# Issuing the next pair's norm, gate and channel attention between the groups of the running pair's attention

## The chip, the core and the metric

One core of a Trainium2 chip runs the whole kernel as one program. Its engines work side by side and each takes its own instructions strictly in order: TensorE (PE in the profile; PEld are its weight loads) multiplies matrices into PSUM, VectorE (DVE) and ScalarE (ACT) do elementwise work, GpSimd (POOL) too, and SyncE (SP) issues the DMAs of this kernel. An instruction waits on semaphores for what it needs, and everything behind it on its engine waits with it. PSUM is eight banks of 128 rows by 512 fp32 values. The metric is device time in microseconds (us), the median of several executions; lower is better.

## What is computed

Four layers run one after the other on 8 images of 64 channels and 64 by 64 pixels, in fp32: a selective scan with a gated convolution (layer 0), channel and spatial attention (layer 1), a small network that is trained for two steps inside the kernel (layer 2), and another spatial attention (layer 3). The change is in what the kernel calls its second stage, which is the end of layer 0 and all of layer 1:

```python
# xo: after the scan.  The norm is over the 64 channels of a pixel.
n = channel_norm(xo)                       # (n - mean) / sqrt(var + 1e-6) * g + b
s0..s3 = split(n, 4, channels)             # s_i is max-pooled by 2**i
outs = [upsample(depthwise3x3(s_i), 2**i) for i in 0..3]
x = xo + gelu(mix1x1(concat(outs))) * n    # the gate
energy = x @ x.T                           # 64 x 64, channel attention
out_c = softmax(max(energy) - energy) @ x
q, k, v = wq @ x + bq, wk @ x + bk, wv @ x + bv     # 16, 16 and 64 rows by 4096 pixels
out_s = v @ softmax(q.T @ k).T             # 4096 x 4096, spatial attention
x2 = (gamma_ca * out_c + x) + (gamma_sa * out_s + x)
```

## The kernel before

The stages are four calls in `conv_seq_kernel`. The second is `gate_and_attention` (L1090). It works on pairs of images: two images of 64 channels fill the 128 rows, so a tile `x` of 128 by 4096 holds a pair, and the loop at L1175 runs over four pairs. For each pair three things follow one another.

**The preparation** (L1176 to L1258). `pair_norm` (L127) centres x with a matmul by `cen`, 1024 pixels at a time into a tile of two PSUM banks (`cps`, from the pool `sc`), copies it on VectorE into the bordered tile `pads[0]`, squares it on ScalarE (`sq`) and sums the squares with a matmul into `var` (L144; a bank of the pool `av`). `rstd` comes from VectorE, a ScalarE square root and a VectorE reciprocal. A matmul by `spread` (L156, 16 rows deep) spreads it to all rows (`rps`), VectorE multiplies (L161) and ScalarE scales and shifts (L162). Three rounds of maxima on VectorE (L1188, L1190) fill `pads[1]` to `pads[3]`. `move` (L1134) copies 16 channels at a time with DMAs, six to a tile, so that three rows of the 3 by 3 kernel lie on different partitions of the tiles `mv`; `conv` (L1144) is then three matmuls. The convolutions go from the smallest grid to the largest, each added to the doubled one before it (L1157, L1166); the largest runs in four blocks `j` of 1024 pixels (`cvps0`), each followed by Gelu on ScalarE and a multiplication and an addition on GpSimd (L1219 to L1221). x goes to DRAM (L1225). Then x is transposed (`xTps`), copied (`xT`) and multiplied with itself into `enps` (L1239), and the softmax of the energy becomes the 128 by 128 matrix `cmapT`.

**The projection** (`project`, L852): k and v of the pair into SBUF, from tiles of two banks.

**The attention** (`run`, L884). A block `i` of 512 queries meets 32 blocks `j` of 128 keys, two to a group, so a pair has 8 x 16 = 128 groups, numbered n. Group n issues the scores of its two key blocks (`scores`, L898: matmuls 16 rows deep into a two-bank tile, ScalarE's exponential into `ex`, VectorE's addition into `sum`), and then the products with v of the group before (`values`, L918). At n % 16 = 1 the queries of the next block are made (`qps`), at 2 the block before is divided (`sumps`, a VectorE reciprocal, four more VectorE operations), at 4 it is finished (`fps`, `x2t`, a DMA). There are four `ex` tiles, so two groups' worth.

The order on every engine is made when the program is built: a scheduler follows the order in which the kernel calls things, and pulls an instruction ahead where it reckons that its inputs are there; DMAs are pulled ahead most. [...] PSUM has three pools of two tiles each in this stage: `mm` with single banks (q, `sumps`, `fps`, the small convolutions), `sc` with two banks a tile (scores, `cps`, `rps`, `cvps0`, `xTps`, k, v) and `av` with single banks (`av`, `var`, `enps`). That is all eight banks.

Of the kernel before, what the change touches and what calls it, by code (L numbers as in the profile page):

```python
# [17 lines left out]
NB = 8  # L18
C = 64
# [24 lines left out]
class Common:  # L44
# [81 lines left out]

    def pair_norm(self, work, sc, var, src, dst, consts, eps, g, b):  # L127

        nc = self.nc
        cen, avg, spread = consts
        for i in range(NBK // 2):
            ps = sc.tile([128, 2, BK], F32, name="cps", tag="sc")
            for e in range(2):
                nc.tensor.matmul(
                    ps[:, e, :], cen, src[:, bass.ts(2 * i + e, BK)], start=True, stop=True
                )
            nc.vector.tensor_copy(dst(i), ps.rearrange("p e (r c) -> p (e r) c", c=S))
            sq = work.tile([128, 2, BK], F32, name="sq", tag="blk", bufs=3)  # L140
            nc.scalar.activation(sq, ps, AF.Square)
            for e in range(2):
                m = 2 * (NBK - 1 - 2 * i - e)
                nc.tensor.matmul(  # L144
                    var[: 2 * NBK], avg[:, m : m + 2 * NBK], sq[:, e, :],
                    start=(i + e == 0), stop=(2 * i + e == NBK - 1),
                )
        rstd = work.tile([2 * NBK, BK], F32, name="rstd", tag="rstd", bufs=1)
        nc.vector.tensor_scalar(rstd, var[: 2 * NBK], eps, None, ALU.add)
        nc.scalar.activation(rstd, rstd, AF.Sqrt)  # L150
        nc.vector.reciprocal(rstd, rstd)
        for i in range(NBK // 2):
            ps = sc.tile([128, 2, BK], F32, name="rps", tag="sc")
            for e in range(2):
                j = 2 * (2 * i + e)
                nc.tensor.matmul(  # L156
                    ps[:, e, :], spread[:, j : j + 2, :].rearrange("k e c -> k (e c)"), rstd,
                    start=True, stop=True,
                )
            out = dst(i)  # L160
            nc.vector.tensor_tensor(out, out, ps.rearrange("p e (r c) -> p (e r) c", c=S), ALU.mult)  # L161
            nc.scalar.activation(out, out, AF.Identity, bias=b, scale=g)  # L162
# [644 lines left out]
class Attention:  # L807
# [76 lines left out]
    def run(self, p, x, k, v, finish):  # L884
# [68 lines left out]
        for n in range(len(groups) + 5):  # L953
            now = []
            if n < len(groups):
                i, g = groups[n]
                now = [(i, j, scores(i, j)) for j in (2 * g, 2 * g + 1)]
            for one in ahead:
                values(*one)
            ahead = now  # L960
            if n % per == 1 and n > per and n // per + 1 < NBK:
                queries(n // per + 1)
            if n % per == 2 and n > per:
                done[n // per - 1] = divide(n // per - 1)
            if n % per == 4 and n > per:
                finish(n // per - 1, done.pop(n // per - 1))

# [122 lines left out]
def gate_and_attention(cm, xh, w, a, x1, mixes, x2):  # L1090
# [4 lines left out]
    with ExitStack() as ctx:  # L1095
# [79 lines left out]
        for p in range(NB // 2):  # L1175
            x = io.tile([2 * C, L], F32, name="x", tag="x")  # L1176
            nc.sync.dma_start(x, xh[2 * p : 2 * p + 2].rearrange("b c l -> (b c) l"))

            def inner(i):
                return pads[0][:, 1 + 2 * i * rows : 1 + 2 * (i + 1) * rows, 1 : S + 1]  # L1180

            var = avp.tile([128, BK], F32, name="var", tag="av")
            cm.pair_norm(work, sc, var, x, inner, cn, 1e-6, cn_g, cn_b)
            src = pads[0][:, 1 : S + 1, 1 : S + 1]
            for i in range(1, 4):
                n = S // 2**i
                m = one.tile([2 * C, 2 * n, n], F32, name=f"max{i}", tag=f"wide{n}")
                nc.vector.tensor_tensor(m, src[:, :, 0::2], src[:, :, 1::2], ALU.max)  # L1188
                src = pads[i][:, 1 : n + 1, 1 : n + 1]
                nc.vector.tensor_tensor(src, m[:, 0::2, :], m[:, 1::2, :], ALU.max)  # L1190
                for r, t in enumerate(moved[i]):
                    move(i, part * r, t)
            p3 = bank(8, 8)
            conv(p3, 3, moved[3][0], 0, 8)
            d3 = doubled(p3, 8, 8)
            p2 = bank(16, 16)
# [3 lines left out]
            d2 = doubled(u2, 16, 16)  # L1200
            u1 = one.tile([2 * C, 32, 32], F32, name="u1", tag="u1")
            for i in range(2):
                p1 = bank(16, 32)
                conv(p1, 1, moved[1][i], 0, 16)
                add_doubled(u1[:, 16 * i : 16 * i + 16, :], p1, d2[:, 8 * i : 8 * i + 8, :])
            d1 = doubled(u1, 32, 32)
            for j in range(NBK // 2):
                blk = bass.ts(j, 2 * BK)
                t = moved[0][j % 3]
                move(0, 2 * j * rows, t)  # L1210
                p0 = sc.tile([128, 2, BK], F32, name="cvps0", tag="sc")
                for e in range(2):
                    conv(p0[:, e, :].rearrange("p (r c) -> p r c", c=S), 0, t, e * rows, rows)
                t = work.tile([2 * C, 2 * rows, S], F32, name="gt", tag="blk", bufs=3)
                add_doubled(
                    t, p0.rearrange("p e (r c) -> p (e r) c", c=S),
                    d1[:, j * rows : (j + 1) * rows, :],
                )
                nc.scalar.activation(t, t, AF.Gelu, bias=fb)  # L1219
                nc.gpsimd.tensor_tensor(t, t, inner(j), ALU.mult)  # L1220
                nc.gpsimd.tensor_tensor(  # L1221
                    x[:, blk], x[:, blk], t.rearrange("p r c -> p (r c)"), ALU.add
                )

# [3 lines left out]
            en = avp.tile([128, BK], F32, name="enps", tag="av")  # L1228
            for j in range(TQ // 8):
                ps = sc.tile([128, 8, 2 * C], F32, name="xTps", tag="sc")  # L1230
                for i in range(8):
                    nc.tensor.transpose(ps[:, i, :], x[:, bass.ts(8 * j + i, 128)], cm.ident)
                xT = work.tile([128, 8, 2 * C], F32, name="xT", tag="blk", bufs=3)
                if j % 2:
                    nc.scalar.copy(xT, ps)
                else:
                    nc.vector.tensor_copy(xT, ps)
                for i in range(8):
                    nc.tensor.matmul(  # L1239
                        en[:, : 2 * C], xT[:, i, :], xT[:, i, :],  # L1240
                        start=(j + i == 0), stop=(8 * j + i == TQ - 1),
                    )
            lo, tot = (work.tile([2 * C, 1], F32, name=n, tag=n) for n in ("lo", "tot"))
            for r in halves:
# [9 lines left out]
                )  # L1254
            cmapT = work.tile([2 * C, 2 * C], F32, name="cmapT", tag="cmapT")
            cm.transpose(psum, cmapT, cmap2)
            for e, r in enumerate(halves):
                nc.sync.dma_start(mixes[2 * p + e], cmapT[r, r])  # L1258

# [11 lines left out]
            att.run(p, x, k, v, finish)  # L1271
# [632 lines left out]
```

## Time and profile before

The median of three runs is 12997.07 us (12996.37 to 12998.29). The profiled execution took 12995.36 us; its span, from the first to the last instruction, is 12993.6 us.

| stretch of the span (us) | what | PE busy | DVE busy | ACT busy | mean granted PE clock |
|---|---|---|---|---|---|
| 0 to 7605 | first stage, scan | | | | |
| 7612 to 7720 | preparation of pair 0 | 73.78 | 41.34 | 18.97 | 0.76 |
| 8255 to 8680 | projection and attention of pair 1 | 423.89 | 352.08 | 258.27 | 1.00 |
| 8680 to 8790 | preparation of pair 2, start of its projection | 84.52 | 39.17 | 23.19 | 0.81 |
| 8790 to 9214 | projection and attention of pair 2 | 422.77 | 352.59 | 255.65 | 1.00 |
| 9757 to 12993.6 | third and fourth stage | | | | |

Times of the trace count from the start of the span. In a line of the timeline come the start, the duration of the group of instructions, the engine, the line of the kernel, the operation, what it writes and reads, the shape and the count (x8). A bracket at the end gives the engine's idle time before it and what released it. An fp32 matmul appears as two records, so "x8" of 512 columns are four matmuls. The granted clock is that of TensorE, 1.0 being full speed. A matmul's end is modelled, so starts are the surer reading.

### The profile page before, as it was taken

How to read it: one execution, taken by the hardware profiler on the slowest of the kernel's cores; microseconds unless marked ns; L12 is line 12 of the kernel's file. 1: busy time of each engine (PE TensorE's matmuls, PEld its weight loads, DVE VectorE, ACT ScalarE, POOL GpSimd, SP SyncE). 2: the span in 40 equal slices, each digit the busy share in tenths (PEclk: the TensorE clock that was granted, in tenths of full speed). 3: DMA queues.
4: the chain of work that ended last, by engine and by line, in shares of the span. 5: the costliest groups of instructions: out<-in, count | busy, mean ns of one | idle time of the engine just before them, and what ended most of it. 6: DMA issues, size and time to landing. Idle time of an engine off the chain costs nothing. (4 is left out here: it accounts for less than half of the span.)

```text
span 12993.6 us, 115955 instructions
## 1 busy us (share of the span) xinstructions
PE 11161.9 (86%) x36395; PEld 4115.1 (32%) x36395; DVE 10881.6 (84%) x7636; ACT 7717.6 (59%) x10047; POOL 6754.4 (52%) x3126
## 2 busy tenths in 40 slices
PE   7788888888888888888887779999996768999999
PEld 2233232232232232232232222323324553333332
DVE  5999999999999999999999958677686786766766
ACT  4676675675675666766765536445465674544544
POOL 4877888878888888788788830000003681000000
PEclk8999999999999999999999989999998888999999
DMA  4888888888889888888888830000001100000000
GB/s 164 301 292 291 308 301 293 306 298 303 300 300 309 296 296 308 300 298 305 297 299 304 295 120 6 24 18 11 17 6 66 39 27 23 6 16 17 6 10 6
DMA packets 686280, 2333.69 MB, mean 180 GB/s; under 512 B 98224, under 2 KB 98896, under 8 KB 683088
## 3 DMA queue, kind: packets, MB, share of 16 engines
q1 hardware_dynamic: 685648, 2326.13, 51.8%
q8 instruction: 290, 4.75, 0.1%
q14 instruction: 342, 2.80, 0.1%
HBM read 2240.69 MB, written 76.28 MB: 178 GB/s over the span
## 5 line engine op out<-in xcount | busy, mean ns | idle before, releaser
L614 POOL TENSOR_TENSOR ct<-ct,h 128x1024 f32<-128x1024 f32 x2048 | 4799.6, 2357 | 1447.1 <-DVE h L605 969.2
L642 PE MATMUL yps<-ct,ident 128*128 128x512 f32 x8192 | 4233.9, 652 | 547.3 <-POOL ct L614 545.3
L605 DVE TENSOR_TENSOR_SCAN h<-a,state,bdu 128x1024 f32<-128x1024 f32 x1344 | 3153.8, 2347 | 227.3 <-ACT state L609 26.7
L915 DVE TENSOR_TENSOR sum<-sum,ex 128x1024 f32<-128x1024 f32 x1920 | 2347.9, 1223 | 770.7 <-ACT ex L908 655.6
L908 ACT ACTIVATE ex<-sc 128x1024 f32<-128x1024 f32 x2048 | 1985.1, 1021 | 1529.8 <-PE sc L903 1529.7
L642 PEld LDWEIGHTS yps<-ct,ident 128*128 128x128 f32 x8192 | 1586.9, 205 | 3164.6 <-issue 1959.1
L582 ACT ACTIVATE a<-dt,amat 128x1024 f32<-128x1024 f32 x2048 | 2333.4, 1142 | 18.1 <-POOL dt L535 14.9
L601 DVE TENSOR_TENSOR bdu<-bt,du 128x1024 f32<-128x1024 f32 x1792 | 2194.9, 1225 | 101.4 <-ACT du L561 46.3
L922 PE MATMUL av<-ex,v 128*64 128x512 f32 x8192 | 1987.8, 606 | 0.0
L609 ACT COPY state<-h 128x1 f32<-128x1 f32 x2048 | 382.9, 187 | 2191.1 <-DVE h L605 2189.4
L903 PE MATMUL sc<-q,k 16*128 16x512 f32 (+1 forms) x8192 | 1656.3, 628 | 5.0 <-ACT ex L908 4.4
L605 DVE TENSOR_TENSOR_SCAN h<-a,bdu 128x1024 f32<-128x1024 f32 x448 | 1024.3, 2286 | 83.5 <-ACT state L609 16.7
L922 PEld LDWEIGHTS av<-ex,v 128*64 128x64 f32 x8192 | 498.2, 136 | 1363.9 <-issue 1360.5
L903 PEld LDWEIGHTS sc<-q,k 16*128 16x128 f32 (+1 forms) x8192 | 562.1, 184 | 1078.8 <-ACT ex L908 743.5
L1220 POOL TENSOR_TENSOR gt<-gt,pad 128x1024 f32<-128x1024 f32 x16 | 34.9, 2180 | 1617.5 <-ACT gt L1219 1538.1
L590 POOL TENSOR_TENSOR bt<-bt,dus 128x1024 f32<-128x1024 f32 x256 | 602.9, 2355 | 8.9 <-DMA bt<-bc 8.8
L408 PE MATMUL vps<-pad,convd 128*128 128x512 f32 x1152 | 534.2, 597 | 5.6 <-ACT z L393 5.6
L605 DVE TENSOR_TENSOR_SCAN h<-a,state,bt 128x1024 f32<-128x1024 f32 x192 | 499.5, 2602 | 15.0 <-POOL bt L590 8.2
L1593 DVE RECIPROCAL r<-e 128x512 f32<-128x512 f32 x128 | 420.7, 3323 | 0.0
L637 PE MATMUL yps<-y,ident 128*128 128x512 f32 x384 | 301.7, 917 | 115.6 <-ACT y L623 115.5
L1596 POOL TENSOR_TENSOR r<-r,half 128x512 f32<-128x512 f32 x128 | 162.7, 1271 | 360.9 <-issue 188.0
L582 ACT ACT_TABLE_LOAD x265 | 340.0, 1283 | 4.7
(402 smaller groups left out, 10325.1 us busy)
## 6 DMA issues: line engine op xcount, KB each, us to landing
bt<-bc SPq DMA_DIRECT2D x2048, 512.0 KB
ct<-bc SPq DMA_DIRECT2D x2048, 512.0 KB
x<-x SPq DMA_DIRECT2D x12, 2048.0 KB
bc<-e SPq DMA_DIRECT2D x256, 64.0 KB
zd<-z SPq DMA_DIRECT2D x64, 256.0 KB
z<-zd SPq DMA_DIRECT2D x64, 256.0 KB
x<-x SPq DMA_DIRECT2D x32, 512.0 KB
part<-x SPq DMA_DIRECT2D x128, 128.0 KB
```

What stands on the lines that cost most here:

```text
L408: nc.tensor.matmul(held[0].rearrange("p (r c) -> p r c", c=S), convd[:, t, :], pad[:, j * rows + dy : (j + 1) * rows + dy, dx : dx + S], s ...
L582: nc.scalar.activation(ctl["a", n], ctl["dt"], AF.Exp, scale=amat[:, ctl["k"], n : n + 1])
L590: nc.gpsimd.tensor_tensor(bt, bt, ctl["dus"], ALU.mult)
L601: nc.vector.tensor_tensor(z, bt, ctl["du"], ALU.mult)
L605: nc.vector.tensor_tensor_scan(h[:, flip], a[:, flip], z[:, flip], 0.0 if state is None else state[:, n : n + 1], ALU.mult, ALU.add,)
L614: nc.gpsimd.tensor_tensor(ct, ct, h, ALU.mult)
L642: nc.tensor.matmul(ctl["ps"][:, bass.ts(i, BK)], cm.ident, ct[:, bass.ts(i, BK)], start=False, stop=(n == N - 1),)
L903: nc.tensor.matmul(sc[:, e, :], k[r : r + d, bass.ts(j, 128)], qs[i][r : r + d, :], start=True, stop=True,)
L908: nc.scalar.activation(ex, sc, AF.Exp)
L915: nc.vector.tensor_tensor(sums[i], sums[i], ex, ALU.add)
L922: nc.tensor.matmul(avs[i][r, :], v[:, j, r], ex[:, e, :], start=(j == 0), stop=(j == TQ - 1))
L1593: nc.vector.reciprocal(r[n][s], e[n][:, s])
```

## The change

`pair_norm` and the body of the pair loop down to `cmapT` become a generator, `prepare(p, w, made, at)`, that stops at a `yield` after every small part. The first pair is prepared as before, in one go, with w = 2 (two banks to a tile). For the others, `prepare(p + 1, 1, ...)` is made before the attention of pair p, and `run` calls `between(n)` at the end of each of the 128 groups, which takes it one part further. With w = 1 each tile is one bank of the pool `mm`, so that the score tiles keep theirs. `var` and `enps` are begun only at n % 16 = 4 and take two places of the pool `av`, so that the attention's own `av` tiles keep alternating. What is left of a preparation after the attention would be run through before the next projection.

The parts fall on these groups: the load of x at 0; `cps` with the `var` of the part before at 4 to 11, the last `var` at 12; `rstd` at 13; `rps` with the multiplication and the scaling at 14 to 21; the three rounds of maxima with their moves at 22 to 24; the first two moves of the full grid at 25; the small convolutions at 26 to 29; then for each of four blocks two parts with a convolution and one with Gelu and the GpSimd work, at 30 to 41; `xTps` with the energy of the part before at 52 to 59, the last energy at 60; the softmax at 61; `cmapT` at 62. From 63 to 127 nothing is added.

Small differences besides: with w = 1 the centred x is copied to `pads[0]`, and x transposed to `xT`, on ScalarE each time (before: VectorE, and VectorE and ScalarE in turn). `add_var` and `add_energy` stand one part behind what feeds them, with w = 2 too. The moves for block j of the full grid are called two blocks ahead.

```diff
-    def run(self, p, x, k, v, finish):
+    def run(self, p, x, k, v, finish, between=lambda n: None):
...
             if n % per == 4 and n > per:
                 finish(n // per - 1, done.pop(n // per - 1))
+            if n < len(groups):
+                between(n)
...
+        def tile_of(w, name):
+            if w == 2:
+                return sc.tile([128, 2, BK], F32, name=name, tag="sc")
+            ps = psum.tile([128, BK], F32, name=name, tag="mm")
+            return ps.rearrange("p (w n) -> p w n", w=1)
+
+        def accumulator(name, w):
+            ps = avp.tile([128, BK], F32, name=name, tag="av")
+            if w == 1:
+                avp.tile([128, BK], F32, name=name + "2", tag="av")
+            return ps
...
+        def prepare(p, w, made, at):
             x = io.tile([2 * C, L], F32, name="x", tag="x")
             nc.sync.dma_start(x, xh[2 * p : 2 * p + 2].rearrange("b c l -> (b c) l"))
...
+            while w == 1 and at() != 4:
+                yield
+            var = accumulator("var", w)
...
+            for i in range(NBK // w):
+                ps = tile_of(w, "cps")
+                for e in range(w):
+                    nc.tensor.matmul(
+                        ps[:, e, :], cen, x[:, bass.ts(w * i + e, BK)], start=True, stop=True
+                    )
+                if w == 2:
+                    nc.vector.tensor_copy(inner(i), grid(ps))
+                else:
+                    nc.scalar.copy(inner(i), grid(ps))
+                sqs[i] = work.tile([128, w, BK], F32, name="sq", tag="blk", bufs=3)
+                nc.scalar.activation(sqs[i], ps, AF.Square)
+                if i:
+                    add_var(i - 1)
+                yield
+            add_var(NBK // w - 1)
+            yield
             rstd = work.tile([2 * NBK, BK], F32, name="rstd", tag="rstd", bufs=1)
             nc.vector.tensor_scalar(rstd, var[: 2 * NBK], 1e-6, None, ALU.add)
             nc.scalar.activation(rstd, rstd, AF.Sqrt)
             nc.vector.reciprocal(rstd, rstd)
+            yield
+            for i in range(NBK // w):
+                ps = tile_of(w, "rps")
+                for e in range(w):
+                    j = 2 * (w * i + e)
+                    nc.tensor.matmul(
+                        ps[:, e, :], spread[:, j : j + 2, :].rearrange("k e c -> k (e c)"), rstd,
+                        start=True, stop=True,
+                    )
+                out = inner(i)
+                nc.vector.tensor_tensor(out, out, grid(ps), ALU.mult)
+                nc.scalar.activation(out, out, AF.Identity, bias=cn_b, scale=cn_g)
+                yield
...
-        for p in range(NB // 2):
+        made, place = {}, [0]
+        parts = prepare(0, 2, made, None)
+        for p in range(NB // 2):
+            for _ in parts:
+                pass
+            x, cmapT = made.pop(p)
...
             k, v = att.project(p, x)
-            att.run(p, x, k, v, finish)
+            more = p + 1 < NB // 2
+            parts = prepare(p + 1, 1, made, lambda: place[0]) if more else iter(())
+
+            def between(n, parts=parts):
+                place[0] = n % (TQ // 2)
+                next(parts, None)
+
+            att.run(p, x, k, v, finish, between)
```

The rest of `prepare` holds the lines of before with `yield` between them, in the parts listed above.

## Prediction

> **What bounds the kernel now.** I first cut the span into stretches and read the engines' busy time in each (start:end, length, then PE, PEld, DVE, ACT and POOL busy, granted clock, DMA share, GB/s).
>
> ```profile
> 8145.00:8255.00 110.00, 84.33 (x254) 38.42 (x251) 40.64 (x40) 23.37 (x23) 18.01 (x8) 0.81 0.23 61
> 8255.00:8680.00 425.00, 423.89 (x2186) 130.90 (x2184) 352.08 (x310) 258.27 (x271) 0.00 (x0) 1.00 0.01 5
> ```
>
> In the attention TensorE is never free and at full clock; VectorE is busy 83%, ScalarE 61%. In the preparation nothing is full and the clock falls to 0.81. Next, the timeline where pair 1 begins, for what the change can save:
>
> ```profile
> 8152.72 3.60 PE L136 MATMUL cps<-x,p_cen 128*128 128x512 f32 x8
> ...
> 8254.15 6.17 PE L861 MATMUL kps<-x,sa_wk 128*128 128x512 f32 x14
> ```
>
> From the first `cps` to the first `kps` are 101.4 us. The same two starts are 8682.24 and 8784.56 for pair 2 (102.3), 9211.37 and 9315.50 for pair 3 (104.1): 307.9 in all, 102.6 a pair. Pair 0 stays where it is, and its order on TensorE hardly changes: I cost it at 0 (either end 3 us, for the squares' sums that now stand one part later).
>
> Then the timeline of a group, with the queries of a block behind it:
>
> ```profile
> 8424.94 1.14 PE L903 MATMUL sc<-q,k 16*128 16x512 f32 x8
> 8426.01 1.94 PE L922 MATMUL av<-ex,v 128*64 128x512 f32 x8
> 8427.88 1.12 PE L894 MATMUL qps<-x,sa_wq 128*128 128x512 f32 x2
> 8428.93 1.14 PE L903 MATMUL sc<-q,k 16*128 16x512 f32 x8
> ```
>
> Plain groups take 2.94 and 3.15 us in turn (8403.51, 8406.66, 8409.60), 3.05 on average; with one more matmul 3.99.
>
> **What is added on TensorE.** A 512-column record takes (3.60 - 0.16) / 8 = 0.43 us at full clock. Per pair: `cps`, `var` and `rps` 48 records, 20.6 us; convolutions 60 full records 25.8, six of 256 columns 1.3, six of 64 columns 0.4; transposes 32 x 0.107 ("x8" takes 1.04) = 3.4; energy 64 x 0.115 ("x32" takes 3.84) = 7.4; `cmapT` 0.1. That is 59.0. They come in about 55 runs of one kind; the group above paid 3.99 - 3.05 - 0.86 = 0.08 for its run, `fps` (8438.82 to 8439.88, after a 3.15 group) 0.2; at 0.13 this is 7.2. Together 66 (63 to 70), all on the path, as TensorE has no gap to hide them in. If nothing else happened: 102.6 - 66 = 36 us a pair, 110 in all.
>
> **What makes TensorE wait.** The changed program's own order on each engine shows what stands behind what. I follow it with durations of the trace.
>
> 1. *rstd and scaling, n = 13 to 21.* In the order of ScalarE the scaling of part n stands ahead of the exponentials of group n + 1; it waits for VectorE's multiplication, which stands behind both sums of group n, which wait for its exponentials. That is a ring.
>
> ```profile
> 8140.99 1.94 ACT L908 ACTIVATE ex<-sc 128x1024 f32<-128x1024 f32 x2 [1.21 <-PE sc L903]
> ...
> 8142.05 2.55 DVE L915 TENSOR_TENSOR sum<-sum,ex 128x1024 f32<-128x1024 f32 x2 [0.60 <-ACT ex L908]
> ```
>
> From exponential to sum 1.06, two sums 2.55, multiplication of one bank 0.66 (the same at L337), scaling of one bank 0.81 (L338), handovers 0.1: 5.2 us a turn, against 3.99 for TensorE, whose next scores wait for a score tile that the exponential frees. At n = 13 ScalarE waits for `rstd` between two table loads of 1.28 and VectorE adds a reciprocal of 3.34: from the scores of n = 12 the scaling of part 14 ends at 16.0 us. Then turns: 15, 16, 17 bring it to 31.3; 18 has the block's reciprocal (3.36) in the ring, 39.8; 19 has the division, two range tests and only half an exponential (5.4), 45.2; 20 has `x2t` (0.74), 51.1; 21 ends at 56.3. The scores of group 22 start about 52.5. Unhindered they would start at 4.0 + 3.05 + 8 x 3.99 + 2.7 (q, `sumps`, `fps`) = 41.6. Wait: 11. The maxima (2.29, 1.23, 0.69, 0.43, 0.29, 0.23) then stand between sums, and the four `ex` tiles run out: 2.3 more.
>
> 2. *The moves, n = 26.* Two dozen DMAs lie between the first maxima and the smallest convolution, and SP issues them one by one:
>
> ```profile
> 8184.08 40.48 SPq L1138 DMA_DIRECT2D mv<-pad  x48
> ...
> 8196.65 1.23 DVE L1190 TENSOR_TENSOR pad<-max 128x1024 f32<-128x1024 f32 x1
> ...
> 8214.49 25.90 PE L1148 MATMUL cvps<-mv,fw 128*128 128x64 f32 x60 [14.57 <-DMA mv<-pad]
> ```
>
> 8214.49 - 8197.88 = 16.6 us, of which 24 issues of 0.587 are 14.1; pair 0 has 16.7. The order is the same in the changed program. The first maxima are done 4.9 after the last scaling, so the data are there at +21.4; TensorE gets to that convolution after the products of group 25, at +13.7. It waits 7.7 there, and with it all scores behind. `x2` and `x1` writes stand in the same queue, but nothing is waiting for those.
>
> 3. *Gelu, n = 32, 35, 38, 41.* Table load 1.28, Gelu 1.15, table load 1.28 ahead of the next exponentials, 3.7 us of ScalarE against its 1 us of slack a group. The order puts q, `fps` or a third of a convolution there, which covers part; I get 1, 2, 0.5 and 1: 4.5 (2 to 10). GpSimd's 4.5 us a block (2.18 + 2.35) have no other work beside them and end long before n = 52.
>
> 4. *Softmax at 61* : two exponentials that wait for VectorE's minima and reciprocals ahead of the next group's: 1.5. *Projection*: the k copy on VectorE now stands behind the division of the last block (recip 3.36, then 3 us): first `kps` to first scores 16.7 instead of 15.9, and the sums start later: 1.5.
>
> Hidden: the `cps` parts (ScalarE 0.57 + 0.59 beside 1.9 more of TensorE), `xTps`, the x load (four groups ahead), the sums of the eight convolution parts (2.55 + 0.69 of VectorE beside 5.7 of TensorE). If that cover failed, the eight scaling turns show the size: about 1 us a part.
>
> 5. *The clock.* No long wait stands in an attention of before, so the price has to come from two places. After the 14.6 us wait above TensorE ran at half speed to 8220.7 (records 0.85 apart), 6.2 us, 3.1 lost. And at the start of pair 0's attention:
>
> ```profile
> 7738.09 2.54 PE L903 MATMUL sc<-q,k 16*128 16x512 f32 x8 [1.11 <-ACT ex L908]
> 7740.55 3.68 PE L922 MATMUL av<-ex,v 128*64 128x512 f32 x8
> 7744.17 2.09 PE L903 MATMUL sc<-q,k 16*128 16x512 f32 x8
> 7746.19 3.68 PE L922 MATMUL av<-ex,v 128*64 128x512 f32 x8
> 7749.80 1.14 PE L903 MATMUL sc<-q,k 16*128 16x512 f32 x8
> ```
>
> A few waits of 1.1 between scores were enough for 11 us at half speed, 5.5 lost. The wait of step 2 costs 3 to 5.5; steps 1 to 3 may add spells. I take 6 a pair; from 3 (one short spell) to 23 (all eight turns of the ring at half speed, 5.6 for a plain group at half and 1.8 for the part: 7.4 instead of 5.2, 17.6, and a spell of 5.5).
>
> The Trainium skill, "TensorE: Matmul & The Clock Gate", Part 1 (the HAM clock gate), speaks against this change: after an idle window of about 3.4 us the array runs at half clock until it has been busy for about 3.4 us. By that rule only the wait of step 2 would count, with 3.4 us at half speed and 1.7 lost a pair, and the total would be 13 us lower; the row at 7738 went to half speed after waits of only 1.1 and stayed there 11 us, so I go by the rows.
>
> **Sum**, a pair: + 66 + 11 + 2.3 + 7.7 + 4.5 + 1.5 + 1.5 + 6 = 100.5, - 102.6: - 2.1. Three pairs: - 6. Against the profiled execution's 12995.4 us this is **12990 us** (it lay 1.7 under the median of the runs, far inside what counts). The gain of the overlap is handed back as waits. About 0.2%, 26 us, is what a measurement tells from no change.
>
> **Rivals.**
> *A, the buffers cover the ring.* Two score and four `ex` tiles let TensorE run on; only 66, the wait of 7.7 and a clock spell of 3 stay: 76.7, a gain of 26 a pair, 12918. For it: no waits in the attention now, though each reciprocal of 3.36 delays VectorE. Against it: there only sums stand behind VectorE; here exponentials do. Half of it would be 12955.
> *B, the clock gate decides, slower.* Place: the ring, n = 14 to 21, where a quarter of each turn is idle and the inserted matmuls are 16 rows deep; at 8177.8 to 8191.4 sixteen such records ran at half speed without ending it. Price 23 instead of 6: 117.5 a pair, + 15 each, 13040. It turns the sign from 8 us a pair, and passes 0.2% from 17.
> *C, it doesn't overlap* (the scheduler puts the parts back behind the attention): about 12995; the order speaks against it, the parts stand between the groups.
>
> **Chances.** Forecast 0.43, A 0.26, B 0.29, C 0.02. Faster by over 0.2% 0.26 (A), within 0.2% 0.45 (forecast and C), slower by over 0.2% 0.29 (B). The range takes A's near half and B: 12925 to 13045. The forecast's own range, with 63 to 70 for TensorE and a clock price of 3 to 12, is 12970 to 13020.
>
> **What would show it.** First `cps` of a later pair about 14 us after its predecessor's first scores; `kps` right behind the last `fps`. Groups of 5.2 us at n = 14 to 21, releaser of the scores ACT, of the scaling DVE; one wait of 7 to 8 us for a DMA at the 64-column convolution, then records at 0.85. Attentions of pairs 0 to 2 about 510 us from first scores to last `fps`, pair 3's 410. Wrong would be: groups of 4 us there (A), a granted clock well under 0.95 over n = 13 to 41 (B), waits at `cps` or convolutions of the full grid, or at `av` for `var`.

## The result, and the profile after

The changed kernel takes 12992.65 us (median of 12 runs, 12983.43 to 13004.15), the kernel before in the same comparison 12994.37 us; the ratio is 0.9998, with a 95% interval of 0.999 to 1.0006. The profiled execution has a span of 12982.8 us and a run of 12984.6. Forecast were 12990 us and no difference that can be measured.

The overlap does take place. Where pair 1 begins, the timeline of TensorE (start, length, engine, line, operation, tiles) shows the projection right behind the last `fps`, with no preparation between:

```profile
8246.34 1.12 PE L1337 MATMUL fps<-x,cmapT 128*128 128x512 f32 x2
8247.31 5.31 PE L824 MATMUL kps<-x,sa_wk 128*128 128x512 f32 x12
```

The attention that now holds the parts takes more. The windows view gives pair 1 from its first scores to the end of its last `fps`, and the ring's 40 us within it (start:end, length, then PE, PEld, DVE, ACT, POOL busy, granted clock, DMA share, GB/s):

```profile
8263.58:8776.85 513.27, 501.13 (x2327) 153.41 (x2327) 379.72 (x339) 290.75 (x314) 18.14 (x8) 0.96 0.05 13
8331.00:8371.00 40.00, 38.20 (x145) 11.55 (x144) 27.18 (x29) 19.25 (x22) 0.00 (x0) 0.87 0.22 37
```

Before, the same stretch of pair 1 took 412.33 us. The second line is the one to learn from: in the ring TensorE is busy 38.20 of 40 us, and its clock is 0.87. The stage loses time there, but hardly any of it is idle time. The group of the page that waits for exponentials (busy us and mean ns, then the idle time ahead, with what ended most of it) shows only 21.2 us of that over the whole kernel:

```profile
L867 PE MATMUL sc<-q,k 16*128 16x512 f32 (+1 forms) x8192 | 1700.4, 633 | 21.8 <-ACT ex L872 21.2
```

So I split the three attentions that hold parts (first scores to the end of the last `fps`, pairs 0 to 2) with the windows view in stretches of 5 us: idle is length less PE busy, half speed is PE busy times (1 less granted clock), work is the rest, TensorE's time at full clock. The split is not exact: behind a wait the second half of a group's scores waits once more for its own exponential, and the eight `sc` records then read 2.04 us instead of 1.14, all of it busy (8327.82 in the changed kernel). That part counts as work here. Sums of three pairs, in us:

| kernel | length | idle | half speed | work |
|---|---|---|---|---|
| before | 1241.6 | 3.4 | 5.0 | 1233.3 |
| after | 1536.9 | 37.8 | 54.9 | 1444.1 |

The parts bring 210.8 us of work, 34.4 of idle time and 49.9 of half speed: 295.3. What they replace are the stretches from the first `cps` to the first `kps` in the kernel before, 101.4, 101.0 and 101.1 us, 303.6 in all. That saves 8.3 us. With a slower last attention (+1.6) and three projections of 16.27 instead of 15.94 us (+1.0), the stage from the first `kps` to the end of the last `fps` falls from 2023.9 to 2018.2, by 5.7 us.

The ring is there as forecast. All engines of pair 1, in the group with the queries: multiplication (DVE), scaling behind it (ACT), exponentials behind that, sums behind those, and the next multiplication behind the sums:

```profile
8343.27 0.68 DVE L1216 TENSOR_TENSOR pad<-pad,rps 128x512 f32<-128x512 f32 x1
...
8343.98 0.82 ACT L1217 ACTIVATE pad<-pad,cn_b,cn_g 128x512 f32<-128x512 f32 x1 [1.89 <-DVE pad L1216]
8344.70 1.92 ACT L872 ACTIVATE ex<-sc 128x1024 f32<-128x1024 f32 x2
...
8345.74 2.56 DVE L879 TENSOR_TENSOR sum<-sum,ex 128x1024 f32<-128x1024 f32 x2 [1.79 <-ACT ex L872]
...
8348.21 0.68 DVE L1216 TENSOR_TENSOR pad<-pad,rps 128x512 f32<-128x512 f32 x1
```

From one multiplication to the next is a turn of 4.94 us. The wait for the moves and the half-speed records behind it came as forecast too (TensorE and SP's queue; `sc` takes 2.09 instead of 1.14, `av` 3.68 instead of 1.94):

```profile
8385.53 8.80 SPq L1104 DMA_DIRECT2D mv<-pad  x14
...
8395.87 0.85 PE L1114 MATMUL cvps<-mv,fw 128*128 128x64 f32 x6 [3.19 <-DMA mv<-pad]
8396.65 2.09 PE L867 MATMUL sc<-q,k 16*128 16x512 f32 x8
8398.67 3.68 PE L886 MATMUL av<-ex,v 128*64 128x512 f32 x8
```

The square root stands between two table loads and leaves TensorE waiting 1.52 us at 8327.82; the four Gelus of pair 0 leave 0.31, 0.68, 0.31 and 1.64.

### The profile page after: what moved, and what is told of

It is laid out like the page before. It is cut to its first block, busy times and chain, and to the rows that moved or that the text cites. A ratio compares the mean times of both kernels' runs of the same rounds, so it can differ in the third digit from the quotient of the medians.

```text
span 12982.8 us, 115992 instructions
## 1 busy us (share of the span) xinstructions
PE 11190.4 (86%) x36395; PEld 4103.1 (32%) x36395; DVE 10882.1 (84%) x7642; ACT 7771.6 (60%) x10134; POOL 6755.4 (52%) x3126
## 5 line engine op out<-in xcount | busy, mean ns | idle before, releaser
L577 POOL TENSOR_TENSOR ct<-ct,h 128x1024 f32<-128x1024 f32 x2048 | 4800.9, 2358 | 1445.6 <-DVE h L568 973.4
L886 PE MATMUL av<-ex,v 128*64 128x512 f32 x8192 | 2021.2, 615 | 0.0
L867 PE MATMUL sc<-q,k 16*128 16x512 f32 (+1 forms) x8192 | 1700.4, 633 | 21.8 <-ACT ex L872 21.2
L568 DVE TENSOR_TENSOR_SCAN h<-a,bdu 128x1024 f32<-128x1024 f32 x448 | 1024.6, 2287 | 82.7 <-ACT state L572 16.7
```

The lines of the kernel that those rows point to most:

```text
L568: nc.vector.tensor_tensor_scan(h[:, flip], a[:, flip], z[:, flip], 0.0 if state is None else state[:, n : n + 1], ALU.mult, ALU.add,)
L577: nc.gpsimd.tensor_tensor(ct, ct, h, ALU.mult)
L867: nc.tensor.matmul(sc[:, e, :], k[r : r + d, bass.ts(j, 128)], qs[i][r : r + d, :], start=True, stop=True,)
L886: nc.tensor.matmul(avs[i][r, :], v[:, j, r], ex[:, e, :], start=(j == 0), stop=(j == TQ - 1))
```

## The experiments

Theory after the result: the overlap is worth what the work leaves (303.6 - 210.8 = 93 us) and gives it back as short waits and as half speed behind them. Rivals: the gate halves the clock whatever the waits are; or only TensorE's work counts and there is nothing to win back; or part of the effect has nothing to do with the overlap. Ratios are to the kernel before on the same chip. "Stage" is the time from the first `kps` to the end of the last `fps` in one profiled execution (2023.9 before, 2018.2 after), "idle" and "half" are as in the table above.

| run | median us | ratio, 95% | stage | idle | half |
|---|---|---|---|---|---|
| after | 12992.65 | 0.9998 (0.999 to 1.0006) | 2018.2 | 37.8 | 54.9 |
| e1 | 12970.11 | 0.9979 (0.997 to 0.9988) | 1998.0 | 28.9 | 48.3 |
| e2 | 12962.78 | 0.9977 (0.9967 to 0.9986) | 1987.8 | 28.0 | 37.6 |
| e3 | 12971.14 | 0.9983 (0.9974 to 0.9992) | 2010.0 | 39.9 | 51.2 |
| e4 | 12961.22 | 0.9977 (0.9967 to 0.9988) | 1987.3 | 25.9 | 39.6 |
| e5a | 12972.26 | 0.9984 (0.9975 to 0.9993) | 1996.9 | 37.4 | 38.3 |
| e5 | 12957.40 | 0.9975 (0.9965 to 0.9986) | 1980.9 | 29.7 | 29.2 |
| e7 | 12978.45 | 0.9991 (0.9982 to 1.0) | 2008.5 | - | - |
| e8 | 12977.16 | 0.9988 (0.9979 to 0.9997) | 2003.2 | 45.3 | 36.3 |
| e10 | 12926.02 | 0.995 (0.9937 to 0.9964) | 1952.6 | 18.2 | 18.2 |

Work is 1438.0 to 1445.6 us in every kernel of the table with the overlap. Nearly all that differs between their three attentions is idle time and half speed. Each stage is read from one execution; by their intervals, e7 and e8 are not clearly apart from the changed kernel in time, so what is said of them rests on their traces.

### e7: the same parts without the overlap

```diff
-            parts = prepare(p + 1, 1, made, lambda: place[0]) if more else iter(())
+            parts = prepare(p + 1, 2, made, None) if more else iter(())
...
-                next(parts, None)
+                pass
```

> The changed kernel's parts without the overlap: nothing is issued between the groups, and the whole of the next pair's preparation is issued behind the running pair's attention on double banks, as in the kernel before (the sums of squares and the energies stay one block later, the first two moves of the finest scale stay ahead). Theory: the new order inside the preparation is worth nothing by itself, -5 to +5 us of the kernel before. Rival (part of the gain and loss of the change lies in the reordering of the preparation, not in the overlap): more than 5 us off the kernel before.

The theory fell, the rival holds: 13 us under the kernel before, though the interval just reaches no difference. From the last `fps` of a pair to the first scores of the next are 113.51, 113.27 and 113.43 us instead of 117.20, 116.80 and 116.89, 10.7 in all (the other 4.7 of the stage are the half-speed spell at the start of pair 0's attention, which this execution doesn't have). The last sums of squares tell why. Before:

```profile
8165.85 1.12 PE L136 MATMUL cps<-x,p_cen 128*128 128x512 f32 x2
8169.41 3.46 PE L144 MATMUL var<-sq,p_avg 128*16 128x512 f32 x4 [2.43 <-ACT sq L141]
```

and in e7:

```profile
8169.20 1.89 PE L1180 MATMUL var<-sq,p_avg 128*16 128x512 f32 x4
8171.70 1.89 PE L1180 MATMUL var<-sq,p_avg 128*16 128x512 f32 x4 [0.61 <-ACT sq L1196]
```

Issued one block later, the sums no longer wait 2.43 us for their squares, and don't run at half speed behind that. From the first `cps` to the first `rps` pass 21.47 us instead of 25.05. So the new order is worth some 11 us by the trace and 13 by the medians without any overlap. Against that order the overlap shows no gain: in the one execution profiled of each its stage is 10 us longer (2018.2 against 2008.5), part of it spells at the start of attentions that no edit touches. The medians lie 1.7 and 13 us under the kernel before on the same chip, and their intervals overlap, so a loss isn't shown either.

### e2: the wait for the moves

```diff
                 move(0, 2 * j * rows, moved[0][j])
-            yield
+            for _ in range(5 if w == 1 else 1):
+                yield
             p3 = bank(8, 8)
```

> The changed kernel with four more empty parts between the moves and the smallest convolution, about 17 us of attention in which the transfers can land. Theory: TensorE's waits for mv ahead of the smallest convolution (5.37, 3.19 and 2.63 us in the profiled execution) go, and with them the half-speed records right behind (about 3 us per pair): 11 us of wait and up to 9 us of clock, 11 to 20 us in all. If the half-speed time comes from something else it stays: 11 us. Rival (the wait moves: the later convolutions then wait for their own moves, or the xT stage starts late): 0.

The waits for `mv` are gone and the stage is 30.4 us shorter: 9.8 of idle time, 17.3 of half speed and 4.7 by a last attention that began at full clock, which the edit doesn't touch, less 1.5 that work reads higher. Without the 4.7 it is still more than the 20 at most. The theory holds, with a larger term for the clock; the three waits, 11.2 us together, were worth more than twice their length.

### e1, e4, e5a: opening the ring by the order of issue

```diff
             for i in range(NBK // w):
+                if i > 0:
+                    times(i - 1)
+                if i > 1:
+                    scaled(i - 2)
                 ps = tile_of(w, "rps")
...
-                nc.vector.tensor_tensor(out, out, grid(ps), ALU.mult)
-                nc.scalar.activation(out, out, AF.Identity, bias=cn_b, scale=cn_g)
+                rs[i] = ps
                 yield
```

`times` is VectorE's multiplication and `scaled` ScalarE's scaling of one block. e4 is e1 and e2 together; e5a puts `scaled(i - 2)` ahead of `times(i - 1)` and issues no part in each sixteenth group's third.

> The changed kernel with the scaling ring opened: part n issues the multiplication of block n-1, the broadcast of block n and the scaling of block n-2, so that ScalarE no longer waits for VectorE and VectorE no longer waits for TensorE inside one part. Theory (the ring's turn is set by the chain broadcast, multiplication, scaling, exponentials): the turn falls from 4.95 us to TensorE's about 4.0 us, 8 turns, and the half-speed records inside the ring mostly go with it; the term of 11 us per pair goes, so 7 to 11 us per pair, 20 to 33 us in all below the changed kernel. Rival (the clock gate decides, whatever waits there are): the half-speed time stays or moves to the next pause, 0 to 5 us in all. Rival (only TensorE's added work counts): 0.

> Both edits together: the opened ring, and four more empty parts ahead of the smallest convolution. Theory (the two terms are separate waits): the sum of the two, 30 to 50 us below the changed kernel. Rival (the clock gate decides): much less than the sum, as the half-speed time that is cured in one place shows up in the next, 10 to 20 us. Rival (only TensorE's added work counts): 0.

> The ring alone, opened in the right order: in the trace of e1 every scaling on ScalarE still started within 0.05 us of the end of the next block's multiplication on VectorE (8358.79 after 8358.75), since the scaling of block n-2 was issued behind the multiplication of block n-1 in the same tile. Here the scaling of block n-2 comes first, then the multiplication of block n-1, then the broadcast of block n; and no part is issued in the group of the sums and the reciprocal (each sixteenth group's third), so that the broadcast doesn't wait for a bank behind them. Theory (the ring's chain costs 4.95 us a turn, TensorE's work 4.0): with the chain really open the ring's 8 to 11 us per pair go, 10 us more than e1 in the three pairs, that is 28 to 33 us below the changed kernel. Rival (the half-speed records decide and come with the first pause, whatever the ring does): as e1, about 20 us below the changed kernel. Rival (ring without a price): 0.

All three gained, and none for the reason given. From the first `rps` record of pair 1 to the start of the last block's are 38.0 us in e1 and 38.3 in the changed kernel: the ring is as it was. (In e1's pair 2 they are 35.6, but so they are in e2's pair 1, whose ring is that of the changed kernel: in both, 1.7 us are lost to half speed there instead of 5.1.) The timeline of e5, which has e5a's ring, shows it:

```profile
8325.93 0.68 DVE L1213 TENSOR_TENSOR pad<-pad,rps 128x512 f32<-128x512 f32 x1
8326.64 0.82 ACT L1216 ACTIVATE pad<-pad,cn_b,cn_g 128x512 f32<-128x512 f32 x1 [2.31 <-DVE pad L1213]
8327.36 1.92 ACT L872 ACTIVATE ex<-sc 128x1024 f32<-128x1024 f32 x2
```

8326.64 is the first scaling and 8325.93 the first multiplication of the pair, so it is the same block: the scheduler had drawn the scaling ahead of where the program issues it. My reading of e1, that the next block's multiplication held it back, was wrong as well. What e1 and e5a did was to add parts ahead of the convolutions: e1 has no wait for `mv` left, e5a one of 0.92 us. That is e2's cause as far as the traces show it, and e4 gains no more than e2 alone. In e5a, though, idle time is what it was (37.4), since other waits grew (each pair has one of 2.67 or 2.68 us for an exponential), and its gain is half speed alone (54.9 to 38.3).

### e8: the scaling on an idle engine

```diff
-                nc.scalar.activation(out, out, AF.Identity, bias=cn_b, scale=cn_g)
+                if w == 1:
+                    nc.gpsimd.tensor_scalar(out, out, cn_g, cn_b, ALU.mult, ALU.add)
+                else:
+                    nc.scalar.activation(out, out, AF.Identity, bias=cn_b, scale=cn_g)
```

> One edit on the changed kernel: in the overlapped pairs the scaling by gain and bias goes from ScalarE to GpSimd, which is idle there. The traces of e1 and of the ring kernel after it show that the order of issue did not open the ring: each scaling on ScalarE still ran at the end of the same block's multiplication on VectorE (8326.64 behind 8325.93 + 0.68, turns of 4.5 to 5.0 us). On another engine no exponential stands behind a scaling. Theory (the ring's chain sums, multiplication, scaling, exponentials sets the turn of 4.95 us; TensorE's work is 4.0): the turn falls to 4.0 to 4.3 us and the half-speed records inside the ring go; 7 to 11 us per pair, 20 to 33 us in all, or 10 us more than e1's 20 if e1 gained by its empty parts alone. What it costs: GpSimd's scalings are slower (its multiplications of 1024 elements take 2.3 us), so the maxima start some 2 us later and the wait for mv ahead of the smallest convolution grows by as much. Rival (the half-speed time decides and comes with the first pause ahead of the ring): turns stay above 4.6 us, 0 to 10 us in all.

Now the exponentials start beside the scaling, not behind it:

```profile
8342.42 0.78 POOL L1218 TENSOR_SCALAR pad<-pad,cn_g,cn_b 128x512 f32<-128x512 f32 x1 [3.85 <-DVE pad L1216]
8342.51 1.94 ACT L872 ACTIVATE ex<-sc 128x1024 f32<-128x1024 f32 x2 [1.24 <-PE sc L867]
```

From the first to the eighth broadcast of pair 1 pass 30.9 us instead of 38.3, 4.41 a turn with the queries, `sumps` and `fps` in it; all but 1.4 of the 30.9 is TensorE's own work at full clock. The ring cost 7.4 us a pair, 22 in all, its half speed included. But TensorE now comes to the smallest convolution earlier, and finds the transfers no further:

```profile
8384.28 1.52 PE L1114 MATMUL cvps<-mv,fw 128*128 128x64 f32 x6 [7.53 <-DMA mv<-pad]
```

The three waits are 7.23, 7.53 and 7.71 us instead of 5.37, 3.19 and 2.63: 11.3 of the ring's 22 go back at the next wait, more than I had expected. The stage falls by 15.0. The rival (turns above 4.6) is out.

### e3 and e5: table loads

e3 has `AF.Gelu if w == 2 else AF.Identity`, one word in the Gelu's line.

> Leaves out the Gelu of the three overlapped pairs (Identity with the same bias in its place), so that ScalarE loads no table there but those for the square root; everything else as in the changed kernel. Theory: the term for the table loads goes, 4.5 us per pair by the prediction (2 to 10), 13 us in all (6 to 30). The trace of the changed kernel shows waits of TensorE for ex behind the Gelus of 0.3, 0.7, 0.3 and 1.6 us and one half-speed record, which speaks for the lower end. Rival (the exponentials have enough slack to take the loads): 0 to 5 us in all.

The waits for `ex` at the Gelus go, 2.9 us a pair, but idle time doesn't fall: the waits for `mv` are 7.01, 4.83 and 5.98 us in this execution. The stage is 8.2 us shorter, the median 21. Both lie within the theory's 6 to 30, but the profiled execution is the slowest of its eleven (12987.97), and how much of the 21 is the Gelu's, it doesn't tell.

e5 puts the edits of e5a and e2 together, adds epsilon a part earlier, and issues each Gelu in one part with the next convolution.

> All waits taken out that the traces show and that an order of issue can take out: the ring as in e5a, four empty parts ahead of the smallest convolution as in e2, the addition of epsilon a part ahead of the square root (ScalarE waited 1.0 us for it between two table loads), and each Gelu in one part with the next block's convolution, so that TensorE has 2.8 us more work while ScalarE loads tables. Theory (idle time of 11 to 15 us per pair and half-speed time of 16 to 20 us behind it, both caused by the waits): the overlapped attention falls from 512 us to 490 to 495 us, 50 to 65 us in all below the changed kernel, about 12930 us. Rival (the half-speed time comes whatever the waits): only the idle time goes, 8 us per pair, 25 to 30 us in all, no better than e2 and e4 (about 12962 us).

The rival's number came (12957), as the ring had stayed closed. The paired Gelus leave one wait of 2.62 us in place of 0.31, 0.68, 0.31 and 1.64: the last has no convolution beside it and pays for all.

### e6, e9, e12: what a wait costs

```diff
+            if n < len(groups) and dose(n):
+                pause = self.work.tile([128, L], mybir.dt.bfloat16, name="pause", tag="pause", bufs=1)
+                late = now[-1][2][:, 0:1, :].to_broadcast([128, dose(n), BK])
+                nc.scalar.copy(pause.rearrange("p (d n) -> p d n", n=BK)[:, : dose(n), :], late)
```

> The disputed cost by itself. The changed kernel with twenty copies on ScalarE of 512 to 4096 elements a partition (dose 1 to 8; nothing reads what they write), each in the ninth group of a block where no part of the next pair is issued; they hold the exponentials back by about 0.5 us per dose (512 elements take 0.59 us), so that TensorE waits once, by a known amount. Theory (half-speed time is what a wait brings behind it): doses whose wait stays under about 0.8 us cost the wait alone; those above cost the wait and 3 to 5 us of half-speed records, and the spell's length does not grow with the wait; some 50 to 80 us in all. Rival (a wait costs itself and no more; half speed has another cause): the sum of the waits alone, some 20 us.

e6 (12987.91 us, one run) tells nothing of this: its copies read `k`, which is ready when the pair starts, and the scheduler put them all there (7719.4 to 9324.4). It is a second look at the changed kernel, though: a stage of 2019.8 us and 54.1 of half speed, spread otherwise over the pairs (20.0, 19.4 and 14.6 instead of 16.0, 19.5 and 19.4).

> The disputed cost by itself, once more: in e6 nothing tied the copies to their group and all twenty ran at the start of the pair. Here each reads the group's second exponential. The changed kernel with twenty copies on ScalarE of 512 to 4096 elements a partition (0.6 to 3.6 us), each in the ninth group of a block in which no part of the next pair is issued; ScalarE is idle about 1 us in a group of 3 us, so TensorE waits the copy's time less 1 to 2 us, once. Theory: copies that leave a wait under about 0.8 us cost the wait alone; those above cost the wait and a spell of half-speed records of 3 to 5 us, whose length does not grow with the wait. Rival: a wait costs itself and no more.

e9 takes 13005.0 us (one run). Copies of up to 1.9 us leave no wait and no half speed, those of 2.33 us a wait of 0.29 and no half speed. Three waits of 0.71 lost 0, 1.6 and 3.3 us behind them (record lengths less 1.14 for eight `sc`, 2.04 for the eight right behind a wait, and 1.94 for eight `av`), two of 1.57 lost 0 and 4.9. These are the two of 1.57, from the timeline of e9:

```profile
9686.07 2.04 PE L867 MATMUL sc<-q,k 16*128 16x512 f32 x8 [1.57 <-ACT ex L872]
9688.05 1.94 PE L886 MATMUL av<-ex,v 128*64 128x512 f32 x8
9689.91 1.14 PE L867 MATMUL sc<-q,k 16*128 16x512 f32 x8
```

```profile
8708.86 2.60 PE L867 MATMUL sc<-q,k 16*128 16x512 f32 x8 [1.57 <-ACT ex L872]
8711.39 3.68 PE L886 MATMUL av<-ex,v 128*64 128x512 f32 x8
8715.00 2.09 PE L867 MATMUL sc<-q,k 16*128 16x512 f32 x8
8717.02 3.62 PE L886 MATMUL av<-ex,v 128*64 128x512 f32 x8
```

The same wait, once at no price and once with four runs of matmuls at half speed: 0.56 + 1.74 + 0.95 + 1.68 = 4.9 us. Neither expectation holds as it stands: two of the three waits of 0.71 had half speed behind them, and one of the two of 1.57 had none.

> The pauses of e9 with two doses alone, ten copies of 3072 elements (2.75 us, TensorE then waits 0.71 us) and ten of 4096 (3.6 us, wait of 1.57 us), to see how one and the same wait is priced. In e9 three waits of 0.71 lost 0, 1.6 and 3.3 us to half speed behind them and two waits of 1.57 lost 0 and 4.9. Theory (half speed is granted in steps of one fixed length, about 3.3 us, and how a wait falls on the steps decides): every loss is near 0, 1.6, 3.3 or 4.9 us, for both waits, with 0 more frequent at 0.71; twenty waits lose about 40 us in all. Rival (the loss grows with the wait and is otherwise the same each time): one value for each dose, within 0.5 us. Rival (the zeros of e9 are what the rule is, and the losses had another cause): nearly all 0.

e12 takes 13043.85 us (one run). Ten waits of 0.71 lost nothing three times and 1.65 us (1.64 to 1.65) seven times. Ten of 1.57 lost 0 once, 1.65 six times, 3.2 to 3.3 twice, 4.9 once. Nothing lies between the steps. All twenty lost 32.8 us behind 22.8 us of waits. The first theory holds: half speed comes in steps, each 1.65 us lost, and a wait buys none, one, two or three. The rivals, one loss for each length or nearly all 0, are out.

The granted clock in the traces shows more than the record lengths do. It is 1.0 or 0.5, nothing else, and it changes only on a fixed grid of 3.41 us. (A step of 3.41 us at half speed is 1.71 us lost; the record lengths give 1.65.) Here are the stretches around the waits that end at 8174.15 (one step) and 9202.25 (three steps) in e12, cut on that grid:

```profile
8172.57:8175.98 3.41, 2.70 (x13) 0.60 (x8) 2.49 (x3) 3.10 (x4) 0.00 (x0) 1.00 0.00 0
8175.98:8179.39 3.41, 3.41 (x10) 0.77 (x8) 3.15 (x3) 1.39 (x2) 0.00 (x0) 0.50 0.00 0
8179.39:8182.81 3.42, 3.42 (x22) 1.04 (x22) 0.95 (x1) 1.94 (x2) 0.00 (x0) 1.00 0.00 0
9203.39:9213.63 10.24, 10.24 (x28) 2.15 (x26) 5.49 (x6) 3.99 (x4) 0.00 (x0) 0.50 0.00 0
```

Where a wait falls on this grid goes with whether it costs anything. The table gives the time from the last grid point to the start of the wait, for the waits of 0.71 and 1.57 of e9 and e12 and for the 1.11 at the start of an attention in all traces:

| wait | no half speed behind it | one to three steps behind it |
|---|---|---|
| 0.71 | 4 cases, 1.41 to 2.71 us | 9 cases, 3.28 to 3.41 and 0 to 0.90 us |
| 1.11 | 11 cases, 2.57 to 2.75 us | 8 cases, 2.78 to 2.93 and 0.44 to 0.87 us |
| 1.57 | 2 cases, 1.49 and 2.32 us | 10 cases, 2.60 to 3.41 and 0 to 1.05 us |

In each row the two do not mix. No run shifts one wait over the grid on purpose, so this is a rule read from the traces and not an experiment.

### e10: the version that beats both

e8's edit, e2's edit, and two more:

```diff
-            nc.vector.tensor_scalar(rstd, var[: 2 * NBK], 1e-6, None, ALU.add)
-            nc.scalar.activation(rstd, rstd, AF.Sqrt)
+            nc.scalar.activation(rstd, var[: 2 * NBK], AF.Sqrt, bias=eps)
...
-                next(parts, None)
+                if n % (TQ // 2) != 2:
+                    next(parts, None)
```

> The scaling on GpSimd, four empty parts ahead of the smallest convolution, no part in the group of the sums and the reciprocal, and epsilon as the bias of the square root (ScalarE no longer waits 1.0 us for VectorE between two table loads). Left are the waits behind the projection (0.6 to 1.1 us), at the square root (about 0.5) and at the last Gelu (1.6). Theory (waits, each of 1 us or more with a half-speed spell of its own behind it): idle time per pair falls from 11 to 15 us to about 5, half-speed time from 16 to 20 us to about 6; the overlapped attention takes about 490 us instead of 512, 60 to 70 us in all below the changed kernel, about 12925 us. Rival (half speed comes whatever the waits): 500 us a pair and about 12957 us, as the kernel e5 with the same waits but the ring's.

12926.02 us, 1 us off the expected. Pair 1's attention:

```profile
8241.93:8732.15 490.22, 484.30 (x2327) 150.84 (x2327) 379.65 (x338) 285.31 (x306) 27.20 (x16) 0.99 0.05 13
```

Idle time is 6.1 us a pair and half speed 6.1, against 12.6 and 18.3. The stage is 65.6 us shorter than the changed kernel's, more than e2 (30.4) and e8 (15.0) together. With both edits, the 11.3 us that e8 gave back at the moves stay gained; the rest, some 9 us, is left to the two further edits, which were not run alone, and to where the spells fell. Half speed falls with the waits; the rival that it comes anyway is out.

## Why the prediction was right, and where it was wrong

The time (12992.65 against 12990) and the net per pair were right. The sign is right by the stage (5.7 us shorter, 6 forecast); the medians don't tell it from no change. But several terms of the sum were off and cancelled, so that the total came so near is in part luck.

- **Removed**, 102.6 a pair: 101.2. For pairs 2 and 3 I took 8784.56 and 9315.50 as the first `kps`; the runs begin at 8783.27 and 9312.49. The removed time was 4.3 us too large in all.
- **TensorE's work**, 66 (63 to 70): 70.3, at the upper end. All of it is on the path, as forecast. It holds some waiting: six or seven groups a pair have `sc` records of 2.04 us instead of 1.14 behind a wait, some 5 us, which is an estimate; without it the work would be near the 66.
- **Step 1, the ring**, 11 and 2.3 for the maxima: the mechanism was right, each link of it is in the timeline, and the turn shown was 4.94 (forecast 5.2). Taken out in e8 it was worth 7.4. Little of it shows as waits: of the 38.3 us from the first to the eighth broadcast 1.8 are idle and 5.1 lost to half speed. That half speed is not hidden behind the chain: in e2, with the same ring but 1.7 of half speed, pair 1 takes 35.6. So of the 7.4 some 4.7 are the chain's (35.6 - 30.9), and the rest is the clock's.
- **Step 2, the moves**, 7.7: 5.37, 3.19 and 2.63. SP's part was right; TensorE came later than I had it. When e8 let it come on time the wait was 7.23 to 7.71.
- **Step 3, Gelu**, 4.5: 2.9 of waits. **Step 4**, softmax and projection, 3.0: 0.65 us of wait at the transposes and 0.3 at the softmax, and the projection 16.27 us, against 16.7 forecast and 15.94 before.
- **Step 5, the clock**, 6 (3 to 23): this is the term that failed by most, 16.6 a pair. Waits were forecast at 28.5 a pair (steps 1 to 4) and came to 11.5. The two together, 34.5 forecast and 28.1 measured, make up nearly all of what is handed back. I priced single spells behind a few long waits; e9 and e12 show that a wait of 0.7 us may bring one to three steps of 1.65 us, and each pair has eight of 0.6 us or more. My row at 7738 was one wait of 1.11, not a few, and the dearest case of four: the kernel before has the same wait at the start of each attention, and in pair 1 nothing follows it (nor in pair 2; in pair 3 two steps do):

```profile
8272.34 2.04 PE L903 MATMUL sc<-q,k 16*128 16x512 f32 x8 [1.11 <-ACT ex L908]
8274.31 1.94 PE L922 MATMUL av<-ex,v 128*64 128x512 f32 x8
```

- **The Trainium skill** ("TensorE: Matmul & The Clock Gate", Part 1) was weighed and set aside in the prediction, since by its idle window of about 3.4 us only the long wait would count. Waits of 0.71 us decide against that threshold. Its length of a window agrees: the granted clock changes in steps of 3.41 us (e12). The same part, under "A second HAM failure mode: psum-queue depth-cycling", speaks of short idle times between groups of matmuls that make the clock swing; that passage is nearer to this case.
- **Rivals.** A's price is near that of a kernel without most of these waits, 12918 forecast and 12926 in e10, though A kept the wait for the moves, which e10 hasn't, and had less work. B had the right engine and mostly the wrong place: the half speed lies all along the pair, from the first groups to the last Gelu, 16.6 us instead of 23, and 5.1 of it in the ring instead of 17.6. Its sign, a clock under 0.95 over n = 13 to 41, did come (0.92, 0.91 and 0.91), and yet the time didn't rise, as the idle time it counted on top was smaller. C was mispriced: I gave the new order within the later preparations no price, and e7, which is C, takes 12978, not 12995. (Pair 0's own preparation, costed at 0, is 105.7 us from the first `cps` to the first `kps` instead of 104.4.)
- **The sentence "the gain of the overlap is handed back as waits"** holds in its first half. The other half is the slower clock. Against e7, the same order without the overlap, there is no gain to hand back: its stage is 10 us shorter in the one execution of each.

## What to carry to other kernels

Where TensorE is the bound, split a stretch into idle time, time at half clock and work before looking for what is lost: a TensorE that reads as busy can be losing more to its clock than to waits. Small waits in a dense stream cost, on average, more than twice their length (e12: 22.8 us of waits, 32.8 of half speed behind them), and a single one costs anything from its own length to 5 us more, so one row of a trace doesn't give the price. So interleaved work has to be placed so that no in-order engine stands between the stream and its next operand; moving the link to an idle engine did that here (e8), an order of issue does it only if the scheduler keeps it. And run the reordered code once without the overlap: what the overlap is worth is its difference to that, not to the kernel before.

## What the runs showed of the hardware

- The granted clock was 1.0 or 0.5 and changed only on a grid of 3.41 us in every trace of this case. Twenty waits lost 0, 1.65, 3.3 or 4.9 us behind them and nothing between; one and the same wait of 1.57 us lost 0 in one place and 4.9 in another (e12). Which it is goes with the wait's place on the grid (the table under e12).
- Waits of 0.29 to 0.31 us had no half speed behind them (three in e9, two at the Gelus of pair 0 in the changed kernel); waits of 0.71 had it in nine of thirteen cases (e9, e12), and one of 0.60 at the start of pair 1's attention in the changed kernel too. Length is not all: the waits of 0.65 at the transposes of the changed kernel had none, one in each pair.
- GpSimd scaled 512 elements a partition by two columns in 0.78 us, ScalarE in 0.82. Six of 24 took 1.68 or 1.69, all six with VectorE's sums running beside them (e8).
- The records of `rps` and `sc`, both with 16 rows, start 0.01 to 0.02 us apart and lie over one another (8341.50 and 8341.52 in the changed kernel). Nothing is saved by it: a turn of the ring at full clock takes 3.78 us from one `rps` to the next (8331.66 to 8335.44), a plain group of 2.94 and two records of 0.43 come to 3.80.
